# A long convolution with adaptive norms: shared products kept in two PSUM banks, a first block loaded alone, and a residual loaded twice

## The chip, the cores and the metric

The kernel runs on one core of a Trainium2 chip. The metric is the device time of one execution in microseconds. Profiles are of one profiled execution; times in them count from the start of its span. TensorE is called PE (its weight loads PEld), VectorE DVE, ScalarE ACT, GpSimd POOL, and SyncE, which here only issues DMAs, SP.

## The reference, cut to what matters

Input x has 4 batches of 1024 rows of 2048 columns, in fp32. Six modulation rows come from one product with a 2048x12288 matrix. Then a normalised, scaled x goes through a causal convolution along its 2048 columns (one kernel K for all rows), is gated and added to x, and the same is done with a dense layer in the convolution's place.

```python
mod = (_silu(c) @ wmod).reshape(4, 6, 1, -1)
sa, ca, ga, sb, cb, gb = (mod[:, i] for i in range(6))
ga = (2 * (ga >= 0) - 1) * jnp.maximum(jnp.abs(ga), 0.25)   # gb likewise
h = layernorm(x) * (1 + ca) + sa
K = s4_kernel(...)                       # 2048 taps
y = irfft(rfft(h, n=4096) * rfft(K, n=4096), n=4096)[..., :2048]
x = x + ga * (y + D * h)
h = layernorm(x) * (1 + cb) + sb
x = x + gb * (h @ W.T + bias + low_rank_updates(h))
```

## The kernel before, in words

The 4096 rows are 32 blocks of 128 rows. The first stage computes the convolution block by block and stores the result (x1d); the second stage is the dense layer, and fills PE from about 960 us to the end.

**Convolution.** It is a product with a Toeplitz matrix, in tiles of 128 columns. Even and odd tiles of the input are combined so that three half-size products do the work of four: f=0 takes sums of tiles (hs) and is needed by both the even and the odd output; f=2 gives the odd output's remainder; f=1 the even output's. Each operand is held as two fp16 parts (high and low), so each product is three matmuls. A block's output has two halves (q=0, 1), each with 4 tiles even and 4 odd, so each accumulates in one PSUM bank (ya) for even and one (yb) for odd. In the kernel before, for each half: f=0 into ya; ACT copies ya to SBUF (qs, L638); f=2 into yb; DVE adds yb and qs (L642) and multiplies by the gate in SBUF (L644); f=1 adds onto ya; DVE multiplies that by the gate (L651) and adds the residual x (L652). The conv banks, the merge products of stage two's weights (lps, L485, drained by DVE at L487) and others share a pool of five PSUM banks (acc); two more (tps) hold transposes, among them the spread mean and deviation (mrb, L563), and one (mps) the modulation product.

**Operands.** The kernel loads a block's x (conv_load), takes its mean and deviation on ACT (stats, L551 and L554), and for a group of two blocks loads the transposed x in four quarters (quarter_load, L544, tile xq with QS=5 buffers). DVE normalises a quarter for both blocks (quarter_norm, L571), ACT applies scale and shift (quarter_mod, L579, L583), and split makes the fp16 parts (hc, hs; L592 to L599).

**Start.** The modulation matrix comes in six sections of 16 loads of 1 MB (mod_load, L311, two pools wm and wms of two and three buffers, SP's queue), each followed by four matmuls into modps (L316). Section 1 gives the scale ca, section 0 the shift sa, section 2 the gate. Meanwhile `toeplitz` computes K and its fp16 tiles (kh, kl; L283, L284). Blocks 0 and 1 run "early" with the scale alone: their shift is added as the convolution of a row (shift_add, tile gsb, L411), and gate and residual by conv_late, when section 2 is done (mod_gate, L341). `pace` puts one load of sections 0 and 2 after every 2700 columns (ROWC) of conv matmuls. `second` and `third` are generators whose steps run at the ticks of blocks 0 and 1.

**Order.** A scheduler orders the instructions of each engine by their dependences; `tc.issue_after` adds an edge, and `high_priority` moves work forward. [...]PLAN assigns the other work to the ticks of the later blocks: S is a step of the weight merge.

Of the kernel before, what the change touches and what calls it, by code (L numbers as in the profile page):

```python
# [24 lines left out]
P = 128  # L25
# [9 lines left out]
class Net:  # L35
    def __init__(self, ctx, tc, io):
        self.ctx, self.tc, self.nc, self.io = ctx, tc, tc.nc, io
        self.cst = ctx.enter_context(tc.tile_pool(name="cst", bufs=1))
        self.dram = ctx.enter_context(tc.tile_pool(name="scr", bufs=1, space=DRAM))
        self.acc = ctx.enter_context(tc.tile_pool(name="acc", bufs=ACC, space=PSUM))  # L40
        self.tps = ctx.enter_context(tc.tile_pool(name="tps", bufs=TPS, space=PSUM))
        self.mps = ctx.enter_context(tc.tile_pool(name="mps", bufs=1, space=PSUM))

# [32 lines left out]
    def s4(self, pool):  # L76
# [68 lines left out]
        tsc(nl, lam, -1.0, None, MUL)  # L145
        rp = self.tps.tile([P, 8, 16], F32, tag="t", name="s4rp")
        w = 512
        yield
        cps = [[self.acc.tile([P, w], F32, tag="a", name="s4cs") for _ in range(2)] for _ in range(2)]
        for n in range(2):  # L150
# [15 lines left out]
        for n, (cc, sc) in enumerate(cps):  # L166
            tt(wq[n], wr[n], wq[n], ADD)
            v.reciprocal(wq[n], wq[n])
            stt(wr[n], cc, nl[:, 0:1], wq[n], MUL, MUL)
            tt(wi[n], wi[n], wq[n], MUL)  # L170
            yield

            sp = self.acc.tile([16, w], F32, tag="a", name="s4sp")
            for i, x in enumerate((wr[n], wi[n])):
                nc.tensor.matmul(sp, cf[:, i].rearrange("p h v -> p (h v)"), x, start=(i == 0), stop=(i == 1))
            sr = wq[n][0:16]
            nc.scalar.copy(sr, sp)
            for c in range(w // P):
                nc.tensor.transpose(rp[:, 4 * n + c], sr[:, ds(P * c, P)], self.ident[0:16, 0:16])
# [49 lines left out]
        yield  # L229
        kp = self.tps.tile([P, 16], F32, tag="t", name="s4kp")  # L230
        for c in range(2):
# [5 lines left out]
    def toeplitz(self, pool):  # L237
# [25 lines left out]
        ev, od = kv[:, :, 0, :], kv[:, :, 1, :]  # L263
        self.kf = {}
        for f in (0, 2, 1):
            self.kf[f] = [self.kpool.tile([P, HC, P], F16, tag=f"k{x}{f}", name=f"k{x}{f}") for x in "hl"]
        for half in range(2):
            m = ds(4 * half, 4)
            for f in (0, 2, 1):
                hi, lo = (x[:, m] for x in self.kf[f])  # L270
# [12 lines left out]
                v.tensor_copy(hi, src)  # L283
                v.tensor_tensor(lo, src, hi, SUB)  # L284
        self.kf = {f: [x.rearrange("p m t -> p (m t)") for x in y] for f, y in self.kf.items()}
        yield

# [35 lines left out]
    def mod_column(self, pool, home, name, plus_one):  # L323

        nc, v = self.nc, self.nc.vector
        row = pool.tile([P, 512], F32, tag="mg0", name="mrow")
        nc.scalar.copy(row, self.modps)
        ps = self.tps.tile([P, 4, P], F32, tag="t", name="mtp")
# [137 lines left out]
    def merge(self, pool, tmp, c):  # L466
# [11 lines left out]
        for h in range(2):  # L478
            for q in range(4):
                ps = self.acc.tile([P, 512], F32, tag="a", name="lps")  # L480
                osl = ds(512 * q, 512)
# [58 lines left out]

    def quarter_load(self, pl, g, q, blocks=(0, 1)):
        t = pl["q"].tile([P, 2, 4, P], F32, tag="xq", name="xq")
        b = slice(blocks[0], blocks[-1] + 1)
        self.nc.sync.dma_start(out=t[:, b], in_=self.io["xT"][g, :, b, ds(4 * q, 4), :])  # L544
        return t

# [11 lines left out]
    def spread(self, sts):  # L558

        ps = self.tps.tile([P, 2, 2, P], F32, tag="t", name="mrb")  # L560
        for b, st in enumerate(sts):
            for i in range(2):
                self.nc.tensor.transpose(ps[:, i, b], st[:, i : i + 1].to_broadcast([P, P]), self.ident)  # L563
        return ps

    def quarter_norm(self, t, ps, blocks=(0, 1)):
        for i, op in enumerate((ADD, MUL)):
            b = slice(blocks[0], blocks[-1] + 1)
            n = len(blocks)
            m = ps[:, i, b].unsqueeze(2).to_broadcast([P, n, 4, P])  # L570
            self.nc.vector.tensor_tensor(t[:, b], t[:, b], m, op)  # L571

# [12 lines left out]
    def split(self, pl, h, t, q):  # L585
# [10 lines left out]
        if q % 2:  # L596
            sl = slice(2 * q - 2, 2 * q + 2)
            nc.scalar.copy(hs[0][:, sl], self.sm)  # L598
            v.tensor_tensor(hs[1][:, sl], self.sm, hs[0][:, sl], SUB)  # L599
# [6 lines left out]
    def conv_mm(self, pl, hs, x, tick, early, pace, y=None):  # L606
# [8 lines left out]

        def family(ps, f, q, first):
            pf = ps.rearrange("p j t -> p (j t)")
            last = 4 * q + 3
            for i in range(last + 1):
                o = P * max(0, i - 4 * q)  # L620
                k0 = P * max(0, 4 * q - i)
                with pace(3 * (512 - o)):
                    for x, z in ((0, 0), (0, 1), (1, 0)):
                        h = hs[x][:, i] if f == 0 else hc[x][:, 2 * i + 2 - f]
                        nc.tensor.matmul(  # L625
                            pf[:, o:512], h, self.kf[f][z][:, ds(k0, 512 - o)],
                            start=first, stop=(i == last and (x, z) == (1, 0)), skip_group_check=True,
                        )
                        first = False
                if i == 3 and q == 1:  # L630
                    tick()

        for q in range(2):
            jj = slice(4 * q, 4 * q + 4)
            pa = self.acc.tile([P, 4, P], F32, tag="a", name="ya")
            family(pa, 0, q, True)
            qs = pl["t"].tile([P, 4, P], F32, tag="qs", name="qs")
            self.lasta = nc.scalar.copy(qs, pa)  # L638
            tick()
            pb = self.acc.tile([P, 4, P], F32, tag="a", name="yb")  # L640
            family(pb, 2, q, True)
            self.lastv = v.tensor_tensor(yv[:, jj, 1, :], pb, qs, ADD)  # L642
            if not early:
                v.tensor_tensor(yv[:, jj, 1, :], yv[:, jj, 1, :], gv[:, jj, 1, :], MUL)  # L644
            tick()
            family(pa, 1, q, False)
            sl = ds(1024 * q, 1024)
            if early:
                nc.scalar.copy(yv[:, jj, 0, :], pa)
            else:  # L650
                v.tensor_tensor(yv[:, jj, 0, :], pa, gv[:, jj, 0, :], MUL)  # L651
                v.scalar_tensor_tensor(y[:, sl], y[:, sl], 1.0, x[:, sl], MUL, ADD, accum_out=sums[:, q : q + 1])  # L652
            tick()
        return y, sums
# [195 lines left out]
def net(ctx: ExitStack, tc: tile.TileContext, io):  # L850
# [10 lines left out]

    left, right, p2 = ExitStack(), ExitStack(), ExitStack()
    pl = {}
# [66 lines left out]
    def qload(g, q):  # L930
        quarters.setdefault(g, []).append(k.quarter_load(pl, g, q))

    def spread(g):
        mr[g] = k.spread([sts.pop(2 * g + i) for i in range(2)])

    def qnorm(g, q, shift=True):
        k.quarter_norm(quarters[g][q], mr[g])
        k.quarter_mod(quarters[g][q], g // 4, q, shift)

# [6 lines left out]
    for _ in section(1, (wms, wmp)):  # L946
# [3 lines left out]
        if n == X0:  # L950
            load(0)
            load(1)
        n += 1
    with tc.issue_after(k.lastw.ins):
        for q in range(4):
            qload(0, q)
    k.early_scale(msm)
    rows = (x for sec in (0, 2) for x in section(sec, (wms, wmp)))
    for r in range(2):
        stats(r)  # L960
    with tc.issue_after(k.last.ins):
        spread(0)
    for q in range(4):
        qnorm(0, q, False)
        split(0, q)
    with tc.issue_after(k.last.ins):
        take(toe, 1)
    take(rows, 2)
    cols = [0]

# [7 lines left out]

    def second():
        for q in range(4):  # L980
            split(1, q)
            qload(1, q)
            yield

    def third():

        for r in (2, 3):
            stats(r)
            yield
        spread(1)  # L990
# [11 lines left out]
    nxt = second()  # L1002
    load(2)
    ys[0] = k.conv_mm(pl, hs.pop(0), xs[0], lambda: take(nxt, 1), True, pace)
    load(3)
    nxt = third()
    ys[1] = k.conv_mm(pl, hs.pop(1), xs[1], lambda: take(nxt, 1), True, pace)
    take(rows, 40)
    k.gat = k.gate_tile(pl["g"], 0)
    take(nxt, 40)  # L1010
# [62 lines left out]
    for r in range(EARLY):  # L1073
        k.conv_late(xs[r], *ys[r], ratio)
        k.conv_post(pl, r, *ys[r])
        load(r + 4)
    stats(4)
# [65 lines left out]
    take(gens[0], 1)  # L1143
    left.close()

    for name in ("v", "o", "e", "g"):
# [94 lines left out]
```

## Time and profile before

| what | value |
|---|---|
| median of three runs | 2177.79 us (2168.63 to 2178.23) |
| profiled execution, own time | 2178.81 us |
| its span | 2177.0 us |
| mean granted PE clock | 0.971 |
| busy PE / PEld | 2045.0 / 976.3 us |
| busy DVE / ACT / POOL | 1324.4 / 990.5 / 6.4 us |
| moved by DMA | 517.6 MB, mean 238 GB/s |

The own time lies 1.8 us over the span and 1.0 us over the median. A PE that is busy for the whole of a window is not necessarily at its peak, and idle time of an engine costs only where another waits for it. A row of the groups gives line, engine, operation, tiles, shapes and count, then busy time and the mean of one, then the idle time before them and what ended it.

### The profile page before, as it was taken

What the parts mean: (1) busy time and instruction counts of PE and PEld (TensorE: products, weight loads), DVE (VectorE), ACT (ScalarE), POOL (GpSimd) and SP (SyncE); (2) the same over time, 40 slices, a digit from 0 to 9 for tenths busy, and PEclk for the clock granted to TensorE, in tenths of its full rate; (3) what the DMA queues carried; (4) which work ended last, traced back from release to release, by engine and by line L of the source; (5) the groups of instructions that cost most, each with busy time, mean ns of one, the idle gap of its engine ahead of it and who ended that gap; (6) DMA issues with size and microseconds to landing.
All of it is one profiled execution on the core that took longest, in us unless ns stands there. A gap on an engine that the chain in (4) does not pass through costs nothing.

```text
span 2177.0 us, 27282 instructions
## 1 busy us (share of the span) xinstructions
PE 2045.0 (94%) x10641; PEld 976.3 (45%) x10641; DVE 1324.4 (61%) x2263; ACT 990.5 (45%) x1503; POOL 6.4 (0%) x17
## 2 busy tenths in 40 slices
PE   5599688999999989899999999999999999999998
PEld 1144344444444444454554554555444444444444
DVE  4546689989999898956656556556433323232323
ACT  2333777776887778764555445555200000000000
POOL 0000000000000000000000000000000000000000
PEclk8689899999999999999999999999999999999999
DMA  9788677788888864577656556556695545555552
GB/s 384 307 357 304 237 267 259 263 316 300 317 338 302 288 228 171 216 303 289 239 176 236 198 189 236 185 212 218 225 352 191 173 165 164 175 166 163 162 167 72
DMA packets 144784, 517.59 MB, mean 238 GB/s; under 512 B 14649, under 2 KB 14809, under 8 KB 113679
## 3 DMA queue, kind: packets, MB, share of 16 engines
q1 hardware_dynamic: 143600, 511.11, 65.2%
q10 hardware_dynamic: 526, 2.63, 0.3%
q0 software_dynamic: 528, 2.11, 0.3%
q8 instruction: 83, 1.36, 0.2%
q14 instruction: 47, 0.38, 0.1%
HBM read 360.50 MB, written 155.30 MB: 237 GB/s over the span
## 4 chain that ended last, share of the span: by engine, by line
PE 61%; issue 27%; DVE 5%; DMA 3%; ACT 3%; POOL 0%; SPq 0%; POOLq 0%; ACTq 0%; DVEq 0%
PE fZ L761 23%; PE fX L761 15%; PE fY L761 15%; PE ya L625 3%; PE tp L711 3%; DMA wm<-in_wmod 2%; PE modps L316 1%; PE yb L625 1%; DVE xq L571 1%; ACT xq L579 1%; DMA laf<-in_A 0%; DMA kb<-kd 0%; ACT hc L594 0%; DVE wch L513 0%; ACT xq L583 0%
## 5 line engine op out<-in xcount | busy, mean ns | idle before, releaser
L761 PEld LDWEIGHTS <-lf 128*128 128x128 f16 x5376 | 526.0, 98 | 620.5 <-issue 0.9
L761 PE MATMUL fZ<-w,lf 128*128 128x512 f16 x2304 | 514.1, 379 | 0.6 <-ACT p L769 0.6
L761 PE MATMUL fX<-w,lf 128*128 128x512 f16 x1536 | 342.1, 379 | 0.0
L761 PE MATMUL fY<-w,lf 128*128 128x512 f16 x1536 | 342.1, 379 | 0.0
L625 PEld LDWEIGHTS <-hc 128*128 128x128 f16 x2304 | 216.6, 99 | 232.7 <-issue 74.4
L625 PE MATMUL ya<-kh,hs 128*128 128x512 f16 (+3 forms) x768 | 201.3, 338 | 41.6 <-ACT hs L598 23.7
L779 DVE TENSOR_TENSOR xo<-xo,gb 128x512 f32<-128x512 f32 x128 | 87.6, 690 | 242.1 <-DMA xo<-x1d 230.6
L625 PE MATMUL ya<-kh,hc 128*128 128x512 f16 (+3 forms) x768 | 195.3, 332 | 9.5 <-ACT qs L638 9.2
L625 PE MATMUL yb<-kh,hc 128*128 128x512 f16 (+3 forms) x768 | 195.0, 332 | 8.7 <-DVE y L642 4.0
L625 PEld LDWEIGHTS <-hs 128*128 128x128 f16 x1152 | 109.2, 101 | 155.9 <-issue 44.8
L769 ACT COPY p<-fZ 128x512 f32<-128x512 f32 x64 | 37.2, 582 | 292.6 <-PE fZ L761 275.4
L571 DVE TENSOR_TENSOR xq<-xq,mrb 128x1024 f32<-128x1024 f32 x128 | 154.2, 1213 | 8.1 <-PE mrb L563 8.0
L769 ACT COPY p<-fX 128x512 f32<-128x512 f32 x32 | 18.7, 586 | 305.4 <-PE fX L761 212.4
L316 PE MATMUL modps<-wm,sct 128*32 128x512 f32 x768 | 121.9, 677 | 37.5 <-DMA wm<-in_wmod 37.4
L713 ACT ACTIVATE gt<-tp,sb,cb 128x256 f32<-128x256 f32 x256 | 123.9, 570 | 65.8 <-PE tp L711 64.3
L579 ACT ACTIVATE xq<-xq,sa,ca 128x256 f32<-128x256 f32 x240 | 124.8, 588 | 31.8 <-DVE xq L571 31.8
L625 PE MATMUL ya<-kl,hs 128*128 128x512 f16 (+3 forms) x384 | 130.0, 338 | 0.0
L625 PE MATMUL ya<-kl,hc 128*128 128x512 f16 (+3 forms) x384 | 127.3, 332 | 0.0
L625 PE MATMUL yb<-kl,hc 128*128 128x512 f16 (+3 forms) x384 | 127.2, 331 | 0.0
L784 DVE TENSOR_TENSOR fin<-fX,gb 128x512 f32<-128x512 f32 x32 | 22.1, 691 | 127.2 <-PE fX L761 127.1
L485 PE MATMUL lps<-lbh,lac 128*128 128x512 f16 x256 | 86.5, 384 | 9.0 <-DVE y L651 4.1
L595 DVE TENSOR_TENSOR hc<-xq,hc 128x512 f16<-128x512 f32 x128 | 86.6, 682 | 13.1 <-ACT hc L594 12.9
(264 smaller groups left out, 2140.5 us busy)
## 6 DMA issues: line engine op xcount, KB each, us to landing
wm<-in_wmod SPq DMA_DIRECT2D x96, 1024.0 KB
lfd<-lf SPq DMA_DIRECT2D x112, 512.0 KB
lf<-lfd SPq DMA_DIRECT2D x112, 512.0 KB
x<-in_x SPq DMA_DIRECT2D x32, 1024.0 KB
xq<-in_xT SPq DMA_DIRECT2D x64, 512.0 KB
x1d<-y SPq DMA_DIRECT2D x32, 1024.0 KB
x<-x1d SPq DMA_DIRECT2D x32, 1024.0 KB
xo<-x1d SPq DMA_DIRECT2D x128, 256.0 KB
```

The source lines that it names most:

```text
L316: self.last = self.nc.tensor.matmul(self.modps[32 * g : 32 * g + 32, :], self.sct[:, j].rearrange("p r b -> p (r b)"), w[:, ds(512 * g, 512)],
L485: nc.tensor.matmul(ps, la[:, x, k, h], y[:, k, osl], start=(n == 0), stop=(n == 5))
L571: self.nc.vector.tensor_tensor(t[:, b], t[:, b], m, op)
L579: self.nc.scalar.activation(x, x, AF.Identity, bias=self.sa[:, c, b : b + 1], scale=self.ca[:, c, b : b + 1])
L595: v.tensor_tensor(hc[1][:, sl], t, hc[0][:, sl], SUB)
L625: nc.tensor.matmul(pf[:, o:512], h, self.kf[f][z][:, ds(k0, 512 - o)], start=first, stop=(i == last and (x, z) == (1, 0)), skip_group_chec ...
L711: nc.tensor.transpose(tp[:, c, r], xs[r][:, ds(P * (c0 + c), P)], self.ident)
L713: nc.scalar.activation(t[:, c0 + c], tp[:, c], AF.Identity, bias=self.sb[:, c0 + c, b : b + 1], scale=self.cb[:, c0 + c, b : b + 1],)
L761: nc.tensor.matmul(ps[name], lf[i][:, k, x, :], wc[i][k // 4][:, k % 4, y, :], start=(first and n == 0), stop=(n == 3 * HC - 1), skip_grou ...
L769: nc.scalar.copy(t, ps[name])
L779: v.tensor_tensor(x, x, self.gbias[:, h], ADD)
L784: v.tensor_tensor(t, cv, self.gbt[:, h], MUL)
```

## The change

The convolution gets four banks of its own in the first stage (pool cps, tags pa and pb with two buffers each); mrb has a bank (mrp), and the second stage's five (acc) open when these close. The merge products use tps. ACT copies the shared product from pa into pb, and PE adds f=2 onto it, so the add on DVE and the tile qs are gone. After the early blocks, both halves' shared products come first. Block 0's quarters are loaded, normalised and scaled alone; block 1's follow. The casts of kh move from DVE to ACT. Loads of x and quarters are placed anew, and x of blocks 0 and 1 is loaded a second time (xl) for conv_late.

```diff
-        self.acc = ctx.enter_context(tc.tile_pool(name="acc", bufs=ACC, space=PSUM))
         self.tps = ctx.enter_context(tc.tile_pool(name="tps", bufs=TPS, space=PSUM))
-        self.mps = ctx.enter_context(tc.tile_pool(name="mps", bufs=1, space=PSUM))
...
-                v.tensor_copy(hi, src)
+                nc.scalar.copy(hi, src)
...
-                ps = self.acc.tile([P, 512], F32, tag="a", name="lps")
+                ps = self.tps.tile([P, 512], F32, tag="t", name="lps")
...
-        ps = self.tps.tile([P, 2, 2, P], F32, tag="t", name="mrb")
+        ps = self.mrp.tile([P, 2, 2, P], F32, tag="mr", name="mrb")
...
+        def shared(q):
+            pa[q] = self.cps.tile([P, 4, P], F32, tag="pa", name="ya")
+            family(pa[q], 0, q)
+            pb[q] = self.cps.tile([P, 4, P], F32, tag="pb", name="yb")
+            self.lasta = nc.scalar.copy(pb[q], pa[q])
+            tick()
+
+        def rest(q):
             jj = slice(4 * q, 4 * q + 4)
-            pa = self.acc.tile([P, 4, P], F32, tag="a", name="ya")
-            family(pa, 0, q, True)
-            qs = pl["t"].tile([P, 4, P], F32, tag="qs", name="qs")
-            self.lasta = nc.scalar.copy(qs, pa)
-            tick()
-            pb = self.acc.tile([P, 4, P], F32, tag="a", name="yb")
-            family(pb, 2, q, True)
-            self.lastv = v.tensor_tensor(yv[:, jj, 1, :], pb, qs, ADD)
-            if not early:
-                v.tensor_tensor(yv[:, jj, 1, :], yv[:, jj, 1, :], gv[:, jj, 1, :], MUL)
-            tick()
-            family(pa, 1, q, False)
...
+            for e, f, ps in ((1, 2, pb[q]), (0, 1, pa[q])):
+                family(ps, f, q)
+                if early:
+                    nc.scalar.copy(yv[:, jj, e, :], ps)
+                else:
+                    self.lastv = v.tensor_tensor(yv[:, jj, e, :], ps, gv[:, jj, e, :], MUL)
...
+        for f, q in ((shared, 0), (rest, 0), (shared, 1), (rest, 1)) if early else (
+            (shared, 0), (shared, 1), (rest, 0), (rest, 1)
+        ):
+            f(q)
...
         if n == X0:
             load(0)
-            load(1)
         n += 1
     with tc.issue_after(k.lastw.ins):
+        quarters[0] = [k.quarter(pl) for _ in range(4)]
         for q in range(4):
-            qload(0, q)
-    k.early_scale(msm)
+            k.quarter_load(quarters[0][q], 0, q, (0,))
+    with tc.high_priority():
+        stats(0)
+        spread(0, (0,))
+        k.early_scale(msm)
...
+    for h in range(2):
+        for q in (2 * h, 2 * h + 1):
+            k.quarter_norm(quarters[0][q], mr[0], (0,))
+        with tc.issue_after(k.mrow.ins), tc.issue_after(k.lastz.ins):
+            take(toe, 1)
+        for q in (2 * h, 2 * h + 1):
+            k.quarter_mod(quarters[0][q], 0, q, False, (0,))
+            split(0, q)
     take(rows, 2)
+    load(1)
+    with tc.issue_after(k.lastw.ins):
+        for q in range(4):
+            k.quarter_load(quarters[0][q], 0, q, (1,))
...
     def second():
+        with tc.issue_after(k.lasts.ins):
+            stats(1)
+        spread(0, (1,))
+        yield
         for q in range(4):
+            qnorm(0, q, False, (1,))
             split(1, q)
-            qload(1, q)
             yield
+        load(2)
+        yield
 
     def third():
-        for r in (2, 3):
-            stats(r)
-            yield
+        for q in range(2):
+            with tc.issue_after(k.lastw.ins):
+                qload(1, q)
...
+    xl = []
+    with tc.issue_after(k.lastw.ins):
+        for r in range(EARLY):
+            load(r + 4)
+        for r in range(EARLY):
+            xl.append(wms.tile([P, D], F32, tag="wm", name="xl"))
+            nc.sync.dma_start(out=xl[r], in_=io["x"][ds(P * r, P), :])
...
     for r in range(EARLY):
-        k.conv_late(xs[r], *ys[r], ratio)
+        k.conv_late(xl[r], *ys[r], ratio)
         k.conv_post(pl, r, *ys[r])
-        load(r + 4)
...
     left.close()
+    ps1.close()
+    k.acc = k.psum(p2l, "acc", ACC)
```

More of the change, by code (lines that the diff above doesn't have):

```diff
@@ L39, in __init__, with psum @@
         self.dram = ctx.enter_context(tc.tile_pool(name="scr", bufs=1, space=DRAM))
-        self.acc = ctx.enter_context(tc.tile_pool(name="acc", bufs=ACC, space=PSUM))
         self.tps = ctx.enter_context(tc.tile_pool(name="tps", bufs=TPS, space=PSUM))
-        self.mps = ctx.enter_context(tc.tile_pool(name="mps", bufs=1, space=PSUM))
+    def psum(self, stack, name, bufs):
+        return stack.enter_context(self.tc.tile_pool(name=name, bufs=bufs, space=PSUM))
     def const(self, name, shape, dt=F32):
@@ L145, in s4 @@
         tsc(nl, lam, -1.0, None, MUL)
-        rp = self.tps.tile([P, 8, 16], F32, tag="t", name="s4rp")
+        rp = self.mrp.tile([P, 8, 16], F32, tag="mr", name="s4rp")
         w = 512
         yield
-        cps = [[self.acc.tile([P, w], F32, tag="a", name="s4cs") for _ in range(2)] for _ in range(2)]
+        cps = [[self.cps.tile([P, w], F32, tag=t, name="s4cs") for t in ("pa", "pb")] for _ in range(2)]
         for n in range(2):
@@ L171, in s4 @@
             yield
-            sp = self.acc.tile([16, w], F32, tag="a", name="s4sp")
+            sp = self.tps.tile([16, w], F32, tag="t", name="s4sp")
             for i, x in enumerate((wr[n], wi[n])):
@@ L229, in s4 @@
         yield
-        kp = self.tps.tile([P, 16], F32, tag="t", name="s4kp")
+        kp = self.mrp.tile([P, 16], F32, tag="mr", name="s4kp")
         for c in range(2):
@@ L263, in toeplitz @@
         ev, od = kv[:, :, 0, :], kv[:, :, 1, :]
-        self.kf = {}
+        kf, self.kf = {}, {}
         for f in (0, 2, 1):
-            self.kf[f] = [self.kpool.tile([P, HC, P], F16, tag=f"k{x}{f}", name=f"k{x}{f}") for x in "hl"]
+            kf[f] = [self.kpool.tile([P, HC, P], F16, tag=f"k{x}{f}", name=f"k{x}{f}") for x in "hl"]
         for half in range(2):
@@ L269, in toeplitz @@
             for f in (0, 2, 1):
-                hi, lo = (x[:, m] for x in self.kf[f])
+                hi, lo = (x[:, m] for x in kf[f])
                 if f == 0:
@@ L282, in toeplitz @@
                         v.tensor_tensor(src[:, 1:], od[:, 0:3], ev[:, 1:4], SUB)
-                v.tensor_copy(hi, src)
+                nc.scalar.copy(hi, src)
                 v.tensor_tensor(lo, src, hi, SUB)
-        self.kf = {f: [x.rearrange("p m t -> p (m t)") for x in y] for f, y in self.kf.items()}
-        yield
+            self.kf = {f: [x.rearrange("p m t -> p (m t)") for x in y] for f, y in kf.items()}
+            yield
     def prep_mod(self, pool):
@@ L326, in mod_column @@
         row = pool.tile([P, 512], F32, tag="mg0", name="mrow")
-        nc.scalar.copy(row, self.modps)
+        self.mrow = nc.scalar.copy(row, self.modps)
         ps = self.tps.tile([P, 4, P], F32, tag="t", name="mtp")
@@ L539, in conv_load, with quarter, quarter_load @@
         return x
-    def quarter_load(self, pl, g, q, blocks=(0, 1)):
-        t = pl["q"].tile([P, 2, 4, P], F32, tag="xq", name="xq")
+    def quarter(self, pl):
+        return pl["q"].tile([P, 2, 4, P], F32, tag="xq", name="xq")
+    def quarter_load(self, t, g, q, blocks=(0, 1)):
         b = slice(blocks[0], blocks[-1] + 1)
         self.nc.sync.dma_start(out=t[:, b], in_=self.io["xT"][g, :, b, ds(4 * q, 4), :])
-        return t
     def stats(self, pl, x):
@@ L558, in spread @@
     def spread(self, sts):
-        ps = self.tps.tile([P, 2, 2, P], F32, tag="t", name="mrb")
-        for b, st in enumerate(sts):
+        ps = self.mrp.tile([P, 2, 2, P], F32, tag="mr", name="mrb")
+        for b, st in sts.items():
             for i in range(2):
@@ L570, in quarter_norm @@
             m = ps[:, i, b].unsqueeze(2).to_broadcast([P, n, 4, P])
-            self.nc.vector.tensor_tensor(t[:, b], t[:, b], m, op)
+            self.lastz = self.nc.vector.tensor_tensor(t[:, b], t[:, b], m, op)
     def quarter_mod(self, t, b, q, shift=True, blocks=(0, 1)):
@@ L597, in split @@
             sl = slice(2 * q - 2, 2 * q + 2)
-            nc.scalar.copy(hs[0][:, sl], self.sm)
+            self.lasts = nc.scalar.copy(hs[0][:, sl], self.sm)
             v.tensor_tensor(hs[1][:, sl], self.sm, hs[0][:, sl], SUB)
@@ L614, in conv_mm, with family @@
         sums = pl["sm"].tile([P, 2], F32, tag="sums", name="sums")
-        def family(ps, f, q, first):
+        def family(ps, f, q):
             pf = ps.rearrange("p j t -> p (j t)")
@@ L626, in family @@
                             pf[:, o:512], h, self.kf[f][z][:, ds(k0, 512 - o)],
-                            start=first, stop=(i == last and (x, z) == (1, 0)), skip_group_check=True,
+                            start=(f == 0 and (i, x, z) == (0, 0, 0)), stop=(i == last and (x, z) == (1, 0)),
+                            skip_group_check=True,
                         )
-                        first = False
                 if i == 3 and q == 1:
                     tick()
-        for q in range(2):
-            jj = slice(4 * q, 4 * q + 4)
-            pa = self.acc.tile([P, 4, P], F32, tag="a", name="ya")
-            family(pa, 0, q, True)
-            qs = pl["t"].tile([P, 4, P], F32, tag="qs", name="qs")
-            self.lasta = nc.scalar.copy(qs, pa)
-            tick()
-            pb = self.acc.tile([P, 4, P], F32, tag="a", name="yb")
-            family(pb, 2, q, True)
-            self.lastv = v.tensor_tensor(yv[:, jj, 1, :], pb, qs, ADD)
-            if not early:
-                v.tensor_tensor(yv[:, jj, 1, :], yv[:, jj, 1, :], gv[:, jj, 1, :], MUL)
-            tick()
-            family(pa, 1, q, False)
[L647 to L653, printed above, removed]
@@ new lines, in conv_mm @@
+        pa, pb = [None] * 2, [None] * 2
+        def shared(q):
[5 more added lines that the diff above has]
+        def rest(q):
+            jj = slice(4 * q, 4 * q + 4)
+            for e, f, ps in ((1, 2, pb[q]), (0, 1, pa[q])):
[4 more added lines that the diff above has]
+                    self.lastv = v.tensor_tensor(yv[:, jj, e, :], ps, gv[:, jj, e, :], MUL)
+                    if e == 0:
+                        sl = ds(1024 * q, 1024)
+                        v.scalar_tensor_tensor(
+                            y[:, sl], y[:, sl], 1.0, x[:, sl], MUL, ADD, accum_out=sums[:, q : q + 1]
+                        )
+                tick()
@@ L860, in pool @@
         return stack.enter_context(tc.tile_pool(name=name, bufs=bufs, side=side, reuse_waits="tile"))
-    left, right, p2 = ExitStack(), ExitStack(), ExitStack()
+    left, right, p2, ps1 = ExitStack(), ExitStack(), ExitStack(), ExitStack()
+    k.cps = k.psum(ps1, "cps", 2)
+    k.mrp = k.psum(ps1, "mrp", 1)
+    k.mps = k.psum(ps1, "mps", 1)
     pl = {}
@@ L930, in qload, with spread, qnorm @@
     def qload(g, q):
[L931 to L938, printed above, removed]
+        quarters.setdefault(g, []).append(k.quarter(pl))
+        k.quarter_load(quarters[g][q], g, q)
+    def spread(g, blocks=(0, 1)):
+        mr[g] = k.spread({b: sts.pop(2 * g + b) for b in blocks})
+    def qnorm(g, q, shift=True, blocks=(0, 1)):
+        k.quarter_norm(quarters[g][q], mr[g], blocks)
+        k.quarter_mod(quarters[g][q], g // 4, q, shift, blocks)
     def split(r, q):
@@ L951, in net @@
             load(0)
-            load(1)
         n += 1
     with tc.issue_after(k.lastw.ins):
+        quarters[0] = [k.quarter(pl) for _ in range(4)]
         for q in range(4):
-            qload(0, q)
-    k.early_scale(msm)
-    rows = (x for sec in (0, 2) for x in section(sec, (wms, wmp)))
-    for r in range(2):
-        stats(r)
[L961 to L967, printed above, removed]
+            k.quarter_load(quarters[0][q], 0, q, (0,))
[3 more added lines that the diff above has]
+        k.early_scale(msm)
+    rows = (x for sec in (0, 2) for x in section(sec, (wms, wmp)))
+    for h in range(2):
[6 more added lines that the diff above has]
+            split(0, q)
     take(rows, 2)
+    load(1)
+    with tc.issue_after(k.lastw.ins):
+        for q in range(4):
+            k.quarter_load(quarters[0][q], 0, q, (1,))
     cols = [0]
@@ L979, in second @@
     def second():
+        with tc.issue_after(k.lasts.ins):
+            stats(1)
+        spread(0, (1,))
+        yield
         for q in range(4):
+            qnorm(0, q, False, (1,))
             split(1, q)
-            qload(1, q)
             yield
+        load(2)
+        yield
     def third():
-        for r in (2, 3):
-            stats(r)
-            yield
+        for q in range(2):
+            with tc.issue_after(k.lastw.ins):
+                qload(1, q)
+        with tc.issue_after(k.lasts.ins):
+            stats(2)
+        load(3)
+        yield
+        for q in range(2, 4):
+            with tc.issue_after(k.lastw.ins):
+                qload(1, q)
+        stats(3)
+        yield
         spread(1)
@@ L1002, in net @@
     nxt = second()
-    load(2)
     ys[0] = k.conv_mm(pl, hs.pop(0), xs[0], lambda: take(nxt, 1), True, pace)
-    load(3)
     nxt = third()
@@ L1008, in net @@
     take(rows, 40)
+    xl = []
+    with tc.issue_after(k.lastw.ins):
+        for r in range(EARLY):
[3 more added lines that the diff above has]
+            nc.sync.dma_start(out=xl[r], in_=io["x"][ds(P * r, P), :])
     k.gat = k.gate_tile(pl["g"], 0)
```

## The prediction

> **What bounds the kernel now.** I read the slices first, then sums over chosen windows, then the waits, the DMA queue and the groups by shape. Slices (a digit is a tenth; 54 us each):
>
> ```profile
> PE   5599688999999989899999999999999999999998
> DVE  4546689989999898956656556556433323232323
> PEclk8689899999999999999999999999999999999999
> DMA  9788677788888864577656556556695545555552
> ```
>
> From slice 18 on PE is full; the change does not touch that part. Before it come two parts, a start-up where PE is half empty and DMA full, and a middle where DVE is as full as PE. Windows (busy of PE, PEld, DVE, ACT, POOL; clock, DMA share, GB/s):
>
> ```profile
> 70.00:80.00 10.00, 2.50 (x10) 0.84 (x14) 8.93 (x14) 8.20 (x20) 0.00 (x0) 0.62 0.25 103
> 80.00:90.00 10.00, 5.55 (x34) 1.92 (x30) 7.84 (x17) 9.07 (x15) 0.00 (x0) 0.84 0.46 153
> 92.00:128.00 36.00, 32.34 (x188) 10.27 (x189) 1.35 (x4) 3.00 (x4) 0.15 (x1) 0.89 1.00 398
> 300.00:900.00 600.00, 554.12 (x3246) 277.96 (x3244) 544.51 (x1049) 458.96 (x715) 0.41 (x1) 0.98 0.76 274
> 960.00:2177.00 1217.00, 1210.81 (x5844) 578.66 (x5842) 556.71 (x722) 348.02 (x504) 0.00 (x0) 1.00 0.57 201
> ```
>
> DMA is saturated to 70 us and again from 92 us, with a hole between. The timeline of SP shows why:
>
> ```profile
> 57.65 0.55 SPq L544 DMA_DIRECT2D xq<-in_xT  x1
> 59.03 0.33 SPq L311 DMA_DIRECT2D wm<-in_wmod  x1
> 83.80 0.55 SPq L544 DMA_DIRECT2D xq<-in_xT  x1
> ```
>
> SP stands 24.4 us at a load of the second group's quarter (waits: SPq L544 <- DVE sm L592), because all five quarter buffers are held; the modulation weights queue behind it. In the middle, PE's own waits (300 to 900 us: total, times, longest):
>
> ```profile
> PE ya L625 <- DVE we L487: 9.4, 2, 6.8
> PE ya L625 <- ACT qs L638: 8.9, 10, 3.2
> PE lps L485 <- DVE y L651: 4.1, 2, 3.7
> PE yb L625 <- DVE y L642: 4.0, 1, 4.0
> PE yb L625 <- DVE y L651: 3.2, 2, 2.2
> ```
>
> With three smaller ones of this kind (1.5, 1.5, 0.5) these are waits for a PSUM bank: 33.1 of PE's 45.9 us idle there. Groups of the same window (count | busy, mean ns):
>
> ```profile
> L571 DVE TENSOR_TENSOR xq<-xq,mrb 128x1024 f32<-128x1024 f32 x88 | 106.3, 1212 | 2.2 <-PE mrb L563 2.2
> L487 DVE SCALAR_TENSOR_TENSOR we<-lps,lsb_i,we 128x512 f32<-128x512 f32 x64 | 46.0, 744 | 6.5 <-PE lps L485 3.2 <-DMA we<-in_WT 3.0
> L642 DVE TENSOR_TENSOR y<-yb,qs 128x512 f32<-128x512 f32 x47 | 32.1, 684 | 4.6 <-PE yb L625 2.6 <-ACT xq L579 1.1 <-ACT qs L638 0.6
> L644 DVE TENSOR_TENSOR y<-y,gat 128x512 f32<-128x512 f32 x46 | 31.5, 684 | 0.1
> L638 ACT COPY qs<-ya 128x512 f32<-128x512 f32 x47 | 26.9, 573 | 13.8 <-PE ya L625 12.8 <-DVE st L73 0.6 <-DVE y L642 0.3
> ```
>
> **What the Trainium skill says.** "PSUM — Partial Sum Buffer", The four PSUM rules: ScalarE writes leave the written-bits alone, and a matmul without the start flag adds wherever an earlier matmul set them. So PE can add onto a copy; no run shows it yet. "ScalarE: Activation LUTs", Step-by-step: PSUM is the nearer port for ScalarE. The trace has only the copy to SBUF (573 ns); I use that. "DMA: Bandwidth & Descriptors", Where 436 GB/s comes from: a ceiling near 435 GB/s; the trace agrees, 398 at share 1.00. "TensorE: Matmul & The Clock Gate", Part 1: an idle PE falls to half clock. The trace agrees: 0.62 at 70 to 80 us.
>
> **The change part by part**, against the profiled execution: span 2177.0, own time 2178.8, 1.0 above the median 2177.8.
>
> *Start of block 0.* First shared matmul: 77.5 us.
> (a) Load x of block 1 (1 MB) and half of the first quarters (1 MB) no longer stand among the first section's loads. At the 386 GB/s of the first 60 us a MB takes 2.7 us; the x counts, the quarters are queued last. The DMA of kb still competes. I take 2 us off the last weight (55.8).
> (b) PE ends the section at 57.8, but mrow (L327) runs at 62.9, since block 1's statistics stand before it on ACT: 5.1 us. They move behind block 0's split; four of the five count, the new casts of kb being close.
> (c) From the column (64.65) to the scales (71.76) DVE interleaves norms of 1.2 us; they become 128x512, 0.68 each: about 1.8 us. The modulation becomes 32 ACT instructions of 128x128 for 16 of 128x256 (588 ns). The width was not seen; between 0.3 and 0.59 us, I take 0.35, and 1 us saved before the first matmul.
> (d) Six kh casts go from DVE (0.43) to ACT (0.6 as hc, 3.6 us in all). One or two stand before the first operands: 0.6 to 1.2 us lost. These are inside (c)'s stretch.
> Sum 2+4+1.8+1-0.8 = 8, so near 69.5 us.
>
> *New waits in conv 0.* The order of the new program puts two mrb transposes of block 1 on PE's queue within block 0's first shared product. They wait for stats(1), which sits on ACT behind the splits: 1.9 and 2.0 us passes plus small ones. All following matmuls and weights wait behind them: about 6 us. Before, PE lost 6.8 us at 85.5 to a late weight, so this replaces it. The unshared product that began at 94.2 should begin near 85.
>
> *Queue of loads.* The hole of 70 to 90 us is 7.5+5.4 = 12.9 us of DMA. The second group's quarters now come some 15 weights later, when buffers are free. A new hole of about 5 us remains while the transposes hold PE, since weight buffers come free through PE. Bytes before the third section's end are unchanged: 48 weights, 4 x, 4 MB of quarters. So 8 us from the hole, and 2 to 5 from PE being earlier and staying warm: the gate (L341 at 181.7) comes **12 us** earlier; bounds 0 (DMA has no other slack) and 20.
>
> *Residual loaded twice.* Two more MB, 5.3 us at 398 GB/s, after the last of these weights; SP issues 6 DMAs more (0.3 to 0.55 us each, SP has room). Conv_late needs xl some 14 us after the gate; with x of blocks 4 and 5 ahead that is 10.5 us of transfer: covered, just. But xl takes two of the three weight buffers (wms), in which gsb (L411, POOL's queue, landing 9.5 us after issue) had its place: gsb was issued at 165.6, 16 us before the gate, and now waits for the third section's last weight in that pool, some 4 us before the gate, and shares DMA with x and xl. DVE wants it 7 us after the gate, and conv_late, the drains of blocks 2 and 3 and so PE stand behind it. I charge 3 us, bounds 0 and 9. ACT still runs conv_post of blocks 0 and 1 before stats(4), so the chain to block 4 (PE waits 11.3 us at 223) moves with the gate and is not shortened: 12-3 = **9 us** pass on.
>
> *Middle.* DVE loses 64 adds of 684 ns (43.8 us in all, 32.1 in 300 to 900); gating yb straight from PSUM costs what L651 does (681). ACT keeps 64 copies, with four more drains of 0.57 us in blocks 0 and 1. PE keeps every matmul. Conv gets two banks each for ya and yb, and the shared products of both halves run first, so a copy has 4.2 us of other matmuls to hide under (1.6 to 4.2 before), and drains a whole half. What returns: merge products (lps) fall from a share of five banks to two banks, and yb now waits for an ACT copy. Of the 33.1 us I let 13 come back: **20 us** gained. Bounds: 45.9 (all idle) and a loss, below.
>
> *FFN.* Its five banks open after the first stage's close; first needed after the last drains, 0.7 us each: 0 to 3 us, taken as 0; the last left side's transposes stand before it.
>
> Sum: 9+20 = 29, so 2178.8-29 = 2149.8; against the median 2149.
>
> **Rivals.**
> 1. *DVE is the true bound of the middle.* For: DVE 544.5 of 600, full in most windows where PE idles. Then all idle goes, and the start gains 16: 2178.8-46-16 = **2117**. Against: mrb and weight waits stay.
> 2. *Start-up is bound by transfers.* The hole only moves and gsb is late: the start gains 0, the middle 20: **2159**.
> 3. *Copies late.* In the middle, ACT is busy 459 of 600 in strict order, with pieces of 2 us. If each of 60 yb products waits 0.7 us: 42 us, against 9+33: **2179**, no change.
> 4. *Slower: merge products on two banks.* 64 products come in clusters, more of them back to back than before; each third one waits for the first's drain, and all of PE behind it. If half wait for a norm and a drain (1.21+0.74), 32x1.96 = 63 us: 2178.8-42+63 = **2200**. It decides above a mean of 0.7 us for each of the 64. Against: with five banks only 5.6 us of lps waits, and DVE gets lighter.
> That the change does nothing is excluded: the compiled program has 64 fewer adds.
>
> **Numbers.** Forecast 0.48, rivals 0.20, 0.16, 0.08, 0.08. A measurement can tell 0.5% (10.9 us) from nothing. The first three cases are faster but for a few hundredths: 0.83; no change 0.09; slower 0.08. Range 2113 to 2179: from rival 1 with a little more, to rival 3.
>
> **What would show it.** First ya matmul near 69 us; SP without a stall of 24 us; the gate's copy near 170; two short PE waits for st near 75; gsb issued within 5 us of the gate; in 300 to 900 PE idle under 30 us with DVE near 85%; lps waits under 15 us. Wrong if lps waits for we exceed 40 us, if yb waits on ACT exceed 30, or if the gate stays at 180.

## The result, and the profile after

The changed kernel takes 2160.69 us (median of ten runs, 2154.94 to 2167.77); the kernel before took 2178.01 beside it (ten runs, 2167.27 to 2183.35). The ratio is 0.9926, 95% interval 0.9906 to 0.9946: about 16 us faster, where 29 were forecast. The profiled execution has a span of 2159.4 us, at a mean granted clock of 0.979.

The page's slices (54 us each, tenths):

```profile
PE   6788799899999988899999999999999999999999
DVE  5437679878988899757556566565433323232323
PEclk8889899999999999999999999999999999999999
DMA  9988758888888766497556455465695545555552
```

The first two slices of PE are fuller; in the middle (slices 6 to 16) DVE has more room, and PE is hardly fuller. The windows (PE, PEld, DVE, ACT, POOL; clock, DMA share, GB/s) measure both:

```profile
70.00:80.00 10.00, 9.43 (x49) 3.14 (x50) 6.51 (x15) 7.33 (x18) 0.00 (x0) 0.80 0.70 267
80.00:90.00 10.00, 10.00 (x73) 3.23 (x70) 5.40 (x10) 6.17 (x15) 0.00 (x0) 1.00 0.98 394
...
300.00:900.00 600.00, 557.44 (x3263) 279.09 (x3261) 530.20 (x1018) 466.83 (x731) 0.64 (x1) 0.98 0.77 275
```

The hole in the transfers is nearly filled: the DMA shares of the two windows were 0.25 and 0.46 and are now 0.70 and 0.98. The middle shows what went wrong: DVE was busy for 14 us less, and PE gained only 3 (554.1 to 557.4). SP's timeline shows the requeued quarters (x2 is two of them in a row), and no wait for a quarter's buffer; the longest wait from 55 to 95 us is one of 7.8 us for a weight buffer:

```profile
56.65 29.71 SPq L312 DMA_DIRECT2D wm<-in_wmod  x9
...
95.51 1.29 SPq L547 DMA_DIRECT2D xq<-in_xT  x2
...
103.92 3.04 SPq L547 DMA_DIRECT2D xq<-in_xT  x2
```

PE's waits from 300 to 900 us (total, times, longest), and the two groups that took the place of L638, L642 and L644:

```profile
PE yb L627 <- ACT yb L643: 19.8, 10, 4.8
PE ya L627 <- DVE y L653: 5.7, 5, 3.3
PE mrb L565 <- DVE st L74: 5.7, 5, 2.1
PE lps L486 <- DVE lac L475: 3.4, 1, 3.4
PE lps L486 <- DVE we L488: 3.2, 4, 1.1
```

```profile
L653 DVE TENSOR_TENSOR y<-yb,gat 128x512 f32<-128x512 f32 x47 | 32.1, 684 | 9.4 <-PE yb L627 9.2
...
L643 ACT COPY yb<-ya 128x512 f32<-128x512 f32 x46 | 26.4, 574 | 6.7 <-PE ya L627 6.5
```

Of the 33.1 us of waits for a PSUM bank, nothing like the old list is left, but one new entry holds 19.8 us: the product on yb waits for ACT's copy. With the drains on ya (5.7) and lps (3.2), PE's waits at PSUM banks still make 28.7. The start did better. The first shared product, and the gate's copy before (first line) and after:

```profile
64.23 0.61 PE L627 MATMUL ya<-kh,hs 128*128 128x512 f16 x1 [3.46 <-ACT hs L600]
```

```profile
181.74 0.68 DVE L341 COPY mg<-modps 128x512 f32<-128x512 f32 x1
168.47 0.69 DVE L342 COPY mg<-modps 128x512 f32<-128x512 f32 x1
```

The first matmul of the second stage comes at 940.79 us (957.18 before), so all that was gained was gained by then.

Where in time? I took the end of the second of DVE's two residual adds in each block (L656, before L652) and compared. Block 2 ends 12.8 us earlier than before, block 4 16.7, block 8 16.6, block 16 16.9, block 20 15.1, block 30 19.9. So the start gave 13 us by block 2 and the middle added a few.

### The profile page after: what moved, and what is told of

It reads as the page before. It is cut to its first block, busy times and chain, and to the rows that moved or that the text cites. A ratio compares the mean times of both kernels' runs of the same rounds, so it can differ in the third digit from the quotient of the medians.

```text
span 2159.4 us, 27224 instructions
## 1 busy us (share of the span) xinstructions
PE 2042.3 (95%) x10641; PEld 971.1 (45%) x10641; DVE 1289.2 (60%) x2201; ACT 1000.4 (46%) x1529; POOL 6.5 (0%) x17
## 4 chain that ended last, share of the span: by engine, by line
PE 71%; DMA 10%; DVE 9%; ACT 8%; issue 2%; SPq 0%; POOL 0%; ACTq 0%; DVEq 0%; POOLq 0%
PE fZ L772 23%; PE fX L772 15%; PE fY L772 15%; PE ya L627 7%; PE yb L627 4%; DMA wm<-in_wmod 3%; PE modps L317 3%; PE tp L722 3%; ACT xq L581 2%; PE lps L486 2%; DMA wcd<-wch 2%; DMA x<-in_x 2%; DVE wch L514 1%; DVE xq L573 1%; DMA we<-in_WT 1%
## 5 line engine op out<-in xcount | busy, mean ns | idle before, releaser
L627 PE MATMUL ya<-kh,hs 128*128 128x512 f16 (+3 forms) x768 | 191.2, 333 | 20.2 <-ACT hs L600 11.4
L573 DVE TENSOR_TENSOR xq<-xq,mrb 128x1024 f32<-128x1024 f32 (+1 forms) x136 | 155.1, 1152 | 11.2 <-PE mrb L565 5.8
L317 PE MATMUL modps<-wm,sct 128*32 128x512 f32 x768 | 126.4, 676 | 26.6 <-DMA wm<-in_wmod 19.1
```

The lines of the kernel that those rows point to most:

```text
L317: self.last = self.nc.tensor.matmul(self.modps[32 * g : 32 * g + 32, :], self.sct[:, j].rearrange("p r b -> p (r b)"), w[:, ds(512 * g, 512)],
L573: self.lastz = self.nc.vector.tensor_tensor(t[:, b], t[:, b], m, op)
L627: nc.tensor.matmul(pf[:, o:512], h, self.kf[f][z][:, ds(k0, 512 - o)], start=(f == 0 and (i, x, z) == (0, 0, 0)), stop=(i == last and (x, ...
```

## The experiments

Each kernel was timed beside the kernel before in five rounds. Its medians were 2176.3 us for the first four, 2173.4 for the next four and 2173.9 for the last four, so the ratios are compared.

**My theory** after these traces: the start is worth some 14 us and is passed on whole; the middle gains little because a copy that PE needs soon stands in ACT's strict order behind pieces that are not urgent. **Rivals:** the two parts disturb each other; DVE, lps or mrb bound the middle in any case, so that the wait for the copy only stands where another would.

### The two parts, each alone

e1_start_only takes the changed kernel and puts back the old conv_mm and pools:

```diff
+        self.acc = ctx.enter_context(tc.tile_pool(name="acc", bufs=ACC, space=PSUM))
...
-            self.lasta = nc.scalar.copy(pb[q], pa[q])
...
+            self.lasta = nc.scalar.copy(qs, pa)
...
+            family(pb, 2, q, True)
+            self.lastv = v.tensor_tensor(yv[:, jj, 1, :], pb, qs, ADD)
...
-    k.cps = k.psum(ps1, "cps", 2)
-    k.mrp = k.psum(ps1, "mrp", 1)
```

> The start edits alone: conv_mm, the PSUM pools, the SBUF copy qs and the add on DVE stay as before. Theory (the start carries nearly all of the gain, and passes it on whole): first ya near 64, gate's copy near 168, time 2164 (2178 minus 14), ratio 0.9935. Rival (the early start is worth little without the new PSUM order, which takes up the slack in conv 0 and conv 1): gate near 175 and time 2172 or more. PE's waits for PSUM banks between 300 and 900 us stay near 33 us under both.

Ratio 0.9935 (0.9921 to 0.9950), 2161.45 us. First ya at 65.96, DVE's copy of the gate sums at 164.0. PE's waits for banks between 300 and 900 us add up to 33.0, as before (33.1).

e2_psum_only takes the kernel before with the pools and conv_mm of the changed one (its diff is the reverse).

> The PSUM edits alone: copy into the second bank, products added onto it, shared products of both halves first, two banks for lps, one for mrb; start, loads and DVE casts as before. Theory (the middle gains only what is left after yb's wait for ACT's copy): 2175, ratio 0.9985, DVE 300 to 900 near 530, yb waits for ACT near 20 us. Rival (the middle is worth its forecast 20 us by itself, and the early start spoils it): 2158, ratio 0.991.

Ratio 0.9982 (0.9973 to 0.9991), 2171.48 us: 4 us. The wait for the copy is there without the early start, with the same size: 19.9 us in 10 times.

The sum of the two, 0.65% and 0.18%, agrees with the whole change (0.74%) within its interval. Nothing shows that they disturb each other.

### The copy: its wait, its load, its engine, its place

e3_no_copy leaves the copy out of blocks 2 to 31:

```diff
-                            start=(f == 0 and (i, x, z) == (0, 0, 0)), stop=(i == last and (x, z) == (1, 0)),
+                            start=((f == 0 or (f == 2 and not early)) and (i, x, z) == (0, 0, 0)), stop=(i == last and (x, z) == (1, 0)),
...
-            self.lasta = nc.scalar.copy(pb[q], pa[q])
+            if early:
+                self.lasta = nc.scalar.copy(pb[q], pa[q])
```

> The changed kernel, but in blocks 2 to 31 the copy is left out: the products of the odd tiles start their own bank, so the shared products are missing from the odd tiles' sums. PE keeps every matmul, ACT loses 60 copies of 0.57 us (34 us). Theory (yb's wait for the copy is what ate the middle's gain): the 20 us of waits go, a few us come back at other waits: 2145, ratio 0.985. Rival (the wait only stands where another wait would stand, for a bank, mrb or lps): 2158, ratio 0.991, with ya<-DVE y, mrb and lps waits grown by what yb lost.

Ratio 0.9738 (0.9721 to 0.9754), 2118.68 us. That is 41 us less than the changed kernel, twice what the wait itself held. It is too much for the theory as I wrote it: taking the copies out also takes 34 us off ACT, and the scheduler made another order from it (block 4 alone is 14.6 us earlier than in the changed kernel). So I separated the wait from the load.

e5_dummy_copy keeps ACT's work and takes only the wait for yb away. The start of the odd tiles' products is changed as in e3_no_copy; the copy becomes:

```diff
-            self.lasta = nc.scalar.copy(pb[q], pa[q])
+            if early:
+                self.lasta = nc.scalar.copy(pb[q], pa[q])
+            else:
+                qs = pl["t"].tile([P, 4, P], F32, tag="qs", name="qs")
+                self.lasta = nc.scalar.copy(qs, pa[q])
```

> The changed kernel, but in blocks 2 to 31 ACT's copy of the shared product goes to an SBUF tile that nobody reads, and the odd tiles' products start their own bank, so the shared products are missing from the odd tiles' sums. ACT's load is that of the changed kernel, and yb waits for nothing of it. Theory (it is the wait for the copy in ACT's order, not the load of the copies on ACT, that costs): yb waits for ACT below 2 us, 2130 to 2142, ratio 0.978 to 0.984. Rival (the run without copies gained from 34 us less of work on ACT): 2155 or more, ratio 0.990.

Ratio 0.9835 (0.9822 to 0.9848), 2137.39 us: inside the theory's range. No wait of yb for ACT is left in the middle. PE's idle time from 300 to 900 falls from 42.6 us to 27.8 (busy 572.21), while ACT does the same copies. So the wait itself costs. Why e3_no_copy gained still more stays open.

e4_copy_dve gives the copy to DVE:

```diff
-            self.lasta = nc.scalar.copy(pb[q], pa[q])
+            self.lasta = nc.scalar.copy(pb[q], pa[q]) if early else v.tensor_copy(pb[q], pa[q])
```

> The changed kernel, but in blocks 2 to 31 the copy is made by DVE instead of ACT. DVE gets 60 x 0.68 us (41 us, 32 of them between 300 and 900, so near 562 of 600 there), ACT loses 34. Theory (the wait comes from a place in an engine's strict order; DVE is fuller than ACT, so its queue is worse): yb waits for DVE 25 us or more, time 2165 to 2185, ratio 0.994 to 1.003. Rival (ACT's long pieces of 2 us are the cause, and DVE's short ones serve the copy sooner): 2150, ratio 0.987.

Ratio 0.9954 (0.9940 to 0.9968), 2165.75 us. Waits of PE in the middle:

```profile
PE yb L627 <- DVE yb L643: 14.6, 7, 3.6
PE ya L627 <- DVE y L653: 10.0, 6, 5.7
...
PE yb L627 <- DVE ln L74: 4.4, 2, 4.0
```

The two yb rows make 19.0 us, fewer than the 25 expected but about the same as on ACT (19.8), and the wait for the drains on ya grows from 5.7 to 10.0. So the wait does not need ACT's long pieces; a fuller engine with shorter pieces makes PE wait as long.

That leaves the place in the order. One stall of the changed kernel shows it. PE's row has the wait in brackets; the rows of ACT before the copy are seven scalings of a later quarter:

```profile
429.29 0.58 PE L627 MATMUL yb<-kh,hc 128*128 128x512 f16 x1 [3.97 <-ACT yb L643]
```

```profile
425.22 3.54 ACT L581 ACTIVATE xq<-xq,sa,ca 128x256 f32<-128x256 f32 x7
428.66 0.58 ACT L643 COPY yb<-ya 128x512 f32<-128x512 f32 x1
```

ACT is never idle in these rows: 3.54 us of scalings stand ahead of 0.58 us that PE waits for, and PE begins its next shared product, the first that could use a later quarter, only at 445.5 us. Over the middle I took the time from the end of the last f=0 matmul of a half to the start of its copy: in the changed kernel a mean of 2.06 us over 46 copies, 12 of them over 3 us, the longest 10.0. In e5_dummy_copy the copies are just as late (2.00 us), and PE does not wait for them.

e6_copy_first changes the place alone:

```diff
-            self.lasta = nc.scalar.copy(pb[q], pa[q])
+            with self.tc.high_priority() if not early else nullcontext():
+                self.lasta = nc.scalar.copy(pb[q], pa[q])
```

> The changed kernel with the copy of blocks 2 to 31 put ahead in the order of work (a priority on this one instruction). Theory: the copy then stands behind fewer pieces on ACT, yb's wait between 300 and 900 us falls from 20 to about 10, 2150, ratio 0.987. Rival (ACT's pieces behind it, operands and statistics, come late instead): same waits in other places, 2160, ratio 0.992.

Ratio 0.9810 (0.9796 to 0.9823), 2132.31 us: 1.2% below the changed kernel, 1.9% below the kernel before, and well below the 2150 of the theory. PE's waits in the middle, its first rows, and the window of the middle:

```profile
PE yb L627 <- ACT yb L644: 6.1, 7, 2.7
PE ya L627 <- DVE y L654: 5.5, 6, 3.2
PE mrb L565 <- DVE st L74: 5.0, 5, 1.4
```

```profile
300.00:900.00 600.00, 574.70 (x3426) 293.81 (x3424) 542.25 (x1043) 485.37 (x760) 0.64 (x1) 0.99 0.80 283
```

The mean time from product to copy falls from 2.06 to 0.76 us, with none over 3. The wait falls by 13.7 us and PE's idle time in the middle by 17.3 (42.6 to 25.3); nothing that was put behind the copy became a new wait of that size. From 180 to 300 us PE is 6.9 us busier as well (93.8 to 100.7). Note DVE: 542 us busy again, as before the change (544.5), while PE's idle time is 25.3 us where it was 45.9. DVE was as full then, and yet not the bound.

The priority also shifts other work: some hundreds of rows of PE's compiled order differ. The next run is a check on how much of the gain is such luck.

e11_start_qs_first puts the same priority on the old copy to SBUF, in e1_start_only:

```diff
+            with self.tc.high_priority() if not early else nullcontext():
                 self.lasta = nc.scalar.copy(qs, pa)
```

> The start edits alone, with the old SBUF copy qs and the add on DVE, and the priority of the run before on the qs copy of blocks 2 to 31. Theory (the priority is worth what waits for the copy, and here only the even tiles' products on ya wait for it, 9 us between 300 and 900): 2150 to 2155, ratio 0.9895, DVE near 544 of 600. Rival (the priority gains by the other order of work as a whole, and the copy into PSUM isn't needed for it): 2137 or less, ratio 0.983.

Ratio 0.9910 (0.9894 to 0.9925), 2154.42 us: some 5 us better than e1_start_only. PE's wait for that copy falls from 9.3 to 6.1 us only; the rest is in other waits. So the priority alone, with an order shuffled in its own way, doesn't bring e6's gain. From 0.9910 to 0.9810 is what the PSUM edits are worth once the copy has its place: 1.0%, 22 us, give or take 5.

### The start, taken apart

e7_stats1_early undoes one part, loading x of block 1 and taking its statistics ahead of block 0's operands:

```diff
         if n == X0:
             load(0)
+            load(1)
...
         stats(0)
+        stats(1)
         spread(0, (0,))
...
-    load(1)
...
-        with tc.issue_after(k.lasts.ins):
-            stats(1)
```

> The changed kernel with one part of the start undone: x of block 1 is loaded within the first section's weights and its statistics run at the start, ahead of block 0's operands; its quarters stay behind, and its transposes stay in conv 0. Theory (ACT's order and the earlier weights carry the start): mrow 4 us later, first ya near 69 to 71 instead of 64, gate's copy 2 to 5 us later than 168, 2164, ratio 0.9935. Rival (the gain of the start comes from the halved norms and from the mended hole in the transfers): first ya near 66, gate at 168, 2160.

Ratio 0.9912 (0.9898 to 0.9926), 2155.64 us. ACT's copy mrow moves from 51.0 to 55.8 and the first ya from 64.23 to 67.40, as the theory says; but the gate's copy stands at 167.1, not later than the changed kernel's 168.5, and the time is not the 2164 that the theory expected. The 3 us by which this part brings block 0's operands forward are real and worth nothing to the end.

e9_requeue_only makes one change to the kernel before; PE's compiled order stays the same to the last instruction:

```diff
             split(1, q)
-            qload(1, q)
             yield
...
         for r in (2, 3):
+            with tc.issue_after(k.lastw.ins):
+                qload(1, 2 * r - 4)
+                qload(1, 2 * r - 3)
             stats(r)
```

> The kernel before with one part of the change alone: the second group's four quarters are issued two by two ahead of the statistics of blocks 2 and 3 in conv 1, some 14 weights later, and nothing else. PE's order is that of before to the last instruction. Theory (the stall of 24 us on SP held up the modulation weights, and the gate waits for these): no long stall on SP, first ya still at 77, gate's copy near 170 instead of 181.7, 2164 to 2167, ratio 0.995. Rival (the start gains through block 0's earlier operands): gate near 180, 2175 or more.

Ratio 0.9934 (0.9917 to 0.9952), 2160.30 us: as much as all of e1_start_only (0.9935). Its windows:

```profile
70.00:80.00 10.00, 1.70 (x5) 0.66 (x6) 9.04 (x15) 7.40 (x18) 0.00 (x0) 0.67 0.97 403
80.00:90.00 10.00, 10.00 (x62) 3.25 (x61) 7.90 (x17) 9.89 (x17) 0.00 (x0) 0.81 0.38 135
```

and DVE's copy of the gate sums:

```profile
169.27 0.68 DVE L341 COPY mg<-modps 128x512 f32<-128x512 f32 x1
```

PE is even emptier than before from 70 to 80 us (1.70 us busy; the first ya comes at 78.30), but DMA is full there (0.97; what is left of the hole is the 0.38 from 80 to 90), and the gate comes 12.5 us earlier.

e10_quarters_early undoes only the requeue in the changed kernel:

```diff
             split(1, q)
+            qload(1, q)
             yield
...
-        for q in range(2):
-            with tc.issue_after(k.lastw.ins):
-                qload(1, q)
...
-        for q in range(2, 4):
-            with tc.issue_after(k.lastw.ins):
-                qload(1, q)
```

> The changed kernel with only the requeue undone: the second group's quarters are issued one by one as block 1's operands are split, as before. Theory: SP stands again for a quarter's buffer while weights queue behind, gate's copy 6 to 10 us later than 168, 2167, ratio 0.996. Rival (block 0 and 1 leave their quarters so early that the buffers are free in time): gate at 168 and 2158 to 2160, ratio 0.992.

Ratio 0.9966 (0.9953 to 0.9979), 2167.83 us. The gate's copy is at 173.28: 4.8 us later than in the changed kernel, still 8.5 earlier than before. SP issues the fifth quarter at 59.42 and the next at 77.64 (before: 57.65 and 83.80), so its stall is shorter by 8 us, as the first group leaves its quarters earlier here. The earlier first group and the requeue are two ways to fill one hole, and their gains don't add.

e8_x_kept drops the second load of x, and with it the earlier place of the loads of blocks 4 and 5:

```diff
-        for r in range(EARLY):
-            load(r + 4)
-        for r in range(EARLY):
-            xl.append(wms.tile([P, D], F32, tag="wm", name="xl"))
-            nc.sync.dma_start(out=xl[r], in_=io["x"][ds(P * r, P), :])
+        xl = [xs[0], xs[1]]
...
         k.conv_post(pl, r, *ys[r])
+        load(r + 4)
```

> The changed kernel with one part undone: the residual x of blocks 0 and 1 is kept in its buffers and not loaded again, and so x of blocks 4 and 5 is loaded only after conv_late. Two MB less are moved. Theory: stats of block 4 wait for their x again, PE stands some 8 us longer for the operands of block 4 near 220, of which the early drains give some back: 2165, ratio 0.994. Rival (as forecast: the chain to block 4 moves with the gate either way): 2158 to 2160, ratio 0.991.

Ratio 0.9914 (0.9900 to 0.9929), 2156.34 us. My theory missed: block 4 is not later (21.2 us ahead of the kernel before, against 16.7 in the changed kernel). The second load, with the earlier loads that it makes room for, is worth nothing that can be told.

e12_copy_first_x_kept joins the last diff with the priority of e6_copy_first.

> The changed kernel with two edits: the priority on the copy, and x of blocks 0 and 1 kept instead of loaded twice. Theory: the second load is worth nothing and the priority its 25 us: 2128 to 2132, ratio 0.980. Rival (with PE earlier, the chain to block 4 does stand out): 2136 to 2140.

Ratio 0.9789 (0.9772 to 0.9806), 2129.27 us, the lowest median of those that leave no work out, though not told apart from e6_copy_first; each is faster than the kernel before and the changed one. From e8_x_kept, which lacks only the priority, to this run it is 1.25%; from the changed kernel to e6_copy_first it was 1.2%. So the priority's gain came twice, in two programs, which speaks against luck of the order.

## Why the prediction was right or wrong

The direction was right and the time lay in the range; the size was nearly twice too large, and one term made most of it. That the total was not further off is luck: the middle gave 16 us less than forecast, and the start 5 more.

- **Middle, 20 us: wrong.** "Of the 33.1 us I let 13 come back" is the failing step. 28.7 came back, and e2_psum_only puts the whole PSUM part at 4 us. I gave a copy "4.2 us of other matmuls to hide under" and worked out no time for which it would stand in ACT's list before it runs. That time was up to 10 us. The trace before had it already: there the copies to SBUF start a mean of 2.8 us after their product, the longest 13.9, and PE's wait for them was the 8.9 us that I read. Rival 3 had this mechanism, with a wait on each of 60 products; it was 10 waits of 2 us, 19.8 where I worked out 42. The text even said that ACT works "in strict order, with pieces of 2 us", and still took it as the lesser case. With the copy in its place the same edits are worth 22 us, near the forecast's 20. That agreement is in part luck: some 7 of the 22 are matmuls that ran faster (PE's busy time falls from 2041.0 us in e11_start_qs_first to 2034.4), and the forecast had no term for these.
- **Rival 1, DVE as the bound: refuted** by e6_copy_first, where PE's idle time in the middle is 25.3 us with DVE at 542 of 600; before it was 45.9 with DVE at 544.5.
- **Rival 4, merge products on two banks: refuted.** They wait 3.2 us for a drain, well under the 15 us named.
- **Rival 2, a start that gains nothing: refuted** by the gate's copy at 168.5 and the 14 us of e1_start_only.
- **Gate, −12: right in size** (13.3), and the hole in the transfers was the right cause. The addition "2 to 5 from PE being earlier" was wrong as a separate term: e9_requeue_only has it all, 12.5 us, with PE no earlier.
- **First ya, 69.5: it came at 64.23.** The terms a and b made 6 us; mrow came 11.9 earlier. In term c I took 0.35 us for a scaling of 128x128; from the starts of those in a row it is about 0.3 (four in 1.28 us). The error is harmless: this path does not set the end.
- **New waits for st in conv 0, 6 us: right in size.** There are two, 5.2 us in all, the longer one of 3.65 before 70.57.
- **gsb, 3 us: not needed.** It was issued at 164.87, 3.6 us before the gate's copy, and landed in 10.4; DVE's first add of it runs at 176.9, with no wait recorded.
- **Passed on, 9 us:** 14 were, since that charge fell away and the gate came a little earlier than forecast.

The rule quoted from the Trainium skill, "PSUM — Partial Sum Buffer", The four PSUM rules, is what the changed kernel rests on, and its trace has the form: in each half PE's f=2 matmuls on yb follow ACT's copy. "ScalarE: Activation LUTs", Step-by-step, with PSUM as the nearer port, gave no shorter copy: 574 ns to PSUM, 573 to SBUF.

**Open:** why e3_no_copy is 1% faster than e5_dummy_copy. ACT's 34 us less and another order of work come together there, and no run parts them.

## What to carry to other kernels

When a change puts a short operation on another engine between two of PE's products, price its place in that engine's list, not its duration: look at what stands ahead of it when its input is ready, and move it forward. A full engine is not yet the bound; ask which wait ends last. At a start that is bound by loads, find the first DMA that stands for a buffer, and try to requeue it before anything else: four moved loads alone gained as much here as all start edits together.

## What the runs showed of the hardware

PE's matmuls got faster where it waited less. Over the whole program, with 10641 matmuls in each, PE's busy time was 2045.0 us before, 2042.3 after and 2034.4 in e6_copy_first, at mean granted clocks of 0.971, 0.979 and 0.982 (that of other executions of the changed kernel is 0.972 to 0.984, of e6_copy_first 0.983 to 0.985). In the middle a 128x512 product on yb took 392 ns on average in the changed kernel and 380 with the copy first. So some 8 us of the last step's gain came from matmuls that ran faster, on top of the shorter waits.

The granted clock shows where. In the middle of the changed kernel it stands at 0.50 in four stretches, 20.4 us in all. This is the second, which begins 0.3 us before the end of the stall shown above; the first product of yb took 0.58 us there:

```profile
429.00:432.40 3.40, 3.11 (x8) 1.14 (x8) 3.33 (x8) 3.40 (x6) 0.00 (x0) 0.50 1.04 370
```

Two of the others begin within pauses of PE, of 3.4 and 4.8 us, and one shortly after a pause of 2.3. With the copy first there are two such stretches, 6.8 us in all. Not every pause has one: the changed kernel's stall of 3.02 us that ends at 498.5 has none. So in these traces the slower matmuls go with pauses of PE; that the pauses cause them is argued from this, as no run changed the pauses alone.
